# Output projection of the attention layer: by head group inside the last query chunk instead of a stage of its own

## The chip, the cores and the metric

The kernel runs on one core of one Trainium2 chip, in one launch. The metric is device time in microseconds. The engines are named as in the profile: PE is TensorE (PEld its weight loads), DVE is VectorE, ACT is ScalarE, POOL is GpSimd, SP is SyncE, which here issues most of the DMAs.

## The reference

A graph network of four layers on 3327 nodes with 128 features. `adj` is a dense 3327 x 3327 matrix of zeros and ones. Every layer adds its result to x after a layer norm and a relu:

```python
h = relu(layernorm(x)); x = x + L0(h, adj)        # two rounds of swish(adj @ h @ W + b)
h = relu(layernorm(x)); x = x + L1(h, adj)        # attention, below
h = relu(layernorm(x)); x = x + L2(h, adj)        # adj @ h, then a GRU cell
h = relu(layernorm(x)); x = x + L3(h, adj)        # two Laplacian products, with 4 nearest neighbours added

def L1(x, adj):                                   # d = 128 "heads" of width h = 8, n = 3327
    q = (x @ Wq.T).reshape(d, n, h)               # k and v alike
    a = einsum('dnh,dmh->dnm', q, k) * d ** -0.5
    a = softmax(a + adj + adj, axis=2)
    out = einsum('dnm,dmh->dnh', a, v)
    return out.reshape(n, h * d) @ Wo.T           # the output projection
```

The reshapes are plain: they don't transpose. The result of head d at query n therefore stands at position d * 3327 + n of one long row, and row r of the reshaped matrix takes 128 positions of that row. So four heads in a row give about 104 whole rows of the projection (103 or 104), and these rows are complete as soon as the four heads have all their queries.

## The kernel before

Almost all of the time is the attention, some 480 to 10036 us of the span. It is cut into seven query chunks of 476 columns (the last, chunk 6, has 471), each of these into 32 groups of four heads, each group into 26 tiles of 128 keys. Tiles are taken in blocks: in chunks 1 to 6 eight triples and one pair to a group. The order of all engines is written out by hand in this part: instructions go to each engine's queue in the order in which the loops emit them.

One block does these steps, in the order that a string gives (`ORDERS`):

- `a`, `A`, `b`, `B`, `c`: score products on PE (`Block.product`, L926) into one of two pairs of PSUM banks (`banks.pair`, which take turns; `c` fills one bank of a pair), and behind each step a sum on DVE (L942) that adds the adjacency tile and writes `p_early`. A letter is two heads of one tile, `c` a single head. When the last sum of a block is queued, one exponential on ACT over all of them follows (L947).
- `l`: three heads of the last tile into the PSUM tile `late`, an exponential on ACT straight from there (L956), and a product with exp(adj) on POOL (L958).
- `W`: weighing (L969), the product of the probabilities with the values, of a tile that lies about seven tiles back, accumulated in the bank `acc`. After a group's last tile DVE copies `acc` to `o4` (L980) and SP stores it to `ot` in DRAM (L985): eight rows of weighted sums and a ninth with the softmax's denominators.

Blocks alternate between two orders; a triple has `aWAWbWBlc` or `cWaWAbWlB`. Since a group has nine blocks, groups alternate too. `events` (L1009) is called after each block for each of its tiles and emits what comes along: the next group's q and v loads at tile 8 (`load_rest`), the next keys at tile 4, in earlier chunks the next chunk's adjacency columns, and POOL's sums of adjacency columns for the degrees.

After the attention comes `tail`, whose order is left to the framework's planner, not written out; the planner may place an instruction far from its place in the program. `tail` first does the output projection in 26 steps: load `o` from `ot`, reciprocal of the denominators (L1187), product (L1188), eight transposes on PE (L1193), copies on ACT (L1194), eight fp32 products with `wo` (L1197, two instructions each), sum with x in `xs_late` (L1198). Pieces of the layer norm (`layernorm_relu`, in pieces given by `CUTS` = 0, 4, 13, 26) follow as their slots are done. Then `adj_product` multiplies with the adjacency matrix (L235), and the GRU cell follows. In `xs_late` row p * 26 + t of x lies in partition p, slot t. The degrees are read (L1202), scaled (L1203) and turned into scale factors (`scales`) between the two. `tail(True)` is a second version for general inputs, in a loop that runs zero times here.

In layer 1's projections (`for r in range(T)`) the column sums of the adjacency's first chunk are made with five products of one column each (`sum_columns`, L304) and stored element by element (`store_sums`).

Of the kernel before, what the change touches and what calls it, by code (L numbers as in the profile page):

```python
# [56 lines left out]
def kernel(  # L57
# [94 lines left out]
    def layernorm_relu(pool, then=None, tmp=None):  # L152
# [20 lines left out]
        return h, in_pieces(piece)  # L173
# [97 lines left out]
    adj16 = dpool.tile([T, P, N], BF16, name="adj16")  # L271
    keyd = dpool.tile([NH // 4, P, NP], F16, name="keyd")
# [243 lines left out]
    for n, t in enumerate(order):  # L516
        kp = rows_of(t)
        if t in kept:
            part_products(acc, n, parts1, t, kept[t], range(len(CS)), False)
            src = kept[t][:kp, : q_chunks[0][1]]  # L520
        else:
            a = early_a.pop(0) if early_a else load_a(t)
            part_products(acc, n, parts1, t, words(a)[:, :, 1], range(len(CS)), False)
            src = a[:kp, : q_chunks[0][1]]
        firsts[t] = doubled(adj_pools[0], src, t, q_chunks[0][1])
        add_to_sum(firsts[t], 0, n == 0)
        if n == 0:
            nc.vector.tensor_reduce(x_max, x1.rearrange("p t d -> p (t d)"), AX.X, ALU.max, apply_absolute_value=True)
        if n == 1:
            bit_limits()  # L530
            nc.gpsimd.dma_start(vd[N * NH : N * NH + 1, :], zero[:1, :EA])
            for end in (qf, kf):
                nc.gpsimd.dma_start(end[:E, N * NH :], zero[:E])
# [42 lines left out]
    class Parting:  # L576
# [8 lines left out]
        def load(self, side):  # L585
            src = SIDES[side][0]
            self.raw[side] = kq0.tile([E * JW, WJ], F32, name="raw")
            nc.sync.dma_start(self.raw[side], self.rows(src, 0))

        def part(self, side, i):  # L590
            if i == 0:
                self.hi[side] = kq0.tile([E * JW, WJ], F16, name="hi")
                self.lo[side] = kq0.tile([E * JW, WJ], F16, name="lo")
# [10 lines left out]
        def at(self, t):  # L604
# [6 lines left out]
            if t == 10:  # L611
                self.load(1)

# [178 lines left out]
    for r in range(T):  # L792
# [30 lines left out]
        if r == 1:  # L823
            dp = ps.tile([P, 512], F32, name="tp")
# [47 lines left out]
    with tc.tile_pool(name="at_in", bufs=1) as a_pool, tc.tile_pool(name="at_p", bufs=4) as p_pool, tc.tile_pool(  # L872
# [114 lines left out]
        with tc.manual_schedule(engines=engines), ExitStack() as ctx_ps:  # L987
# [21 lines left out]
            def events(c, g, t, n, a_in):  # L1009
                nonlocal coming, part, ahead_part, n_stored, k_next  # L1010
                more = n < len(groups)
                if t == 8 and more:
# [30 lines left out]
            coming = part = None  # L1043
            for n, (c, g) in enumerate(groups, 1):
# [10 lines left out]
                for i, size in enumerate(TRIPLES if c else PAIRS):  # L1055
# [9 lines left out]
                    for step in order:  # L1065
# [26 lines left out]
    nc.sync.dma_start(xs, x1d)  # L1092
# [11 lines left out]
    nc.vector.tensor_add(b_rz, b_ih_s, b_hh_s)  # L1104
# [50 lines left out]
    def tail(general):  # L1155
# [13 lines left out]
        with ExitStack() as s:  # L1169
# [6 lines left out]
            h, done = layernorm_relu(pool, halved)  # L1176
            with tc.tile_pool(name="lo", bufs=3) as lo, tc.tile_pool(name="lo_ps", bufs=2, space=PSUM) as ps:
                wo_s = lo.tile([NH, E, D], F32, name="wo_s", bufs=1)
                nc.gpsimd.dma_start(wo_s, wo)
                for t in range(T):  # L1180
                    kp = rows_of(t)
                    o = lo.tile([P, EA, NH], F32, name="o")
                    src = ot.rearrange("e (p t c) -> t p e c", t=T, c=NH)[t]
                    for p0, p1 in ((0, kp),) if kp == P else ((0, 112), (112, kp)):
                        nc.sync.dma_start(o[p0:p1], src[p0:p1])
                    inv = lo.tile([P, NH], F32, name="inv")
                    nc.vector.reciprocal(inv[:kp], o[:kp, E, :])  # L1187
                    nc.vector.tensor_mul(o[:kp, :E, :], o[:kp, :E, :], inv[:kp].unsqueeze(1).to_broadcast([kp, E, NH]))  # L1188
                    oT = lo.tile([NH, E, P], F32, name="oT")
                    for quad in range(2):  # L1190
                        tp = ps.tile([P, 4, P], F32, name="tp")
                        for j in range(4):
                            nc.tensor.transpose(tp[:, j, :kp], o[:kp, 4 * quad + j, :], ident[:kp, :kp])  # L1193
                        nc.scalar.copy(oT[:, 4 * quad : 4 * quad + 4, :kp], tp[:, :, :kp])  # L1194
                    yp = ps.tile([P, D], F32, name="yp")
                    for e in range(E):
                        nc.tensor.matmul(yp[:kp], oT[:, e, :kp], wo_s[:, e, :], start=(e == 0), stop=(e == E - 1))  # L1197
                    nc.vector.tensor_add(xs[:kp, t, :], xs[:kp, t, :], yp[:kp])  # L1198
                    done(t + 1)

            if not general:
                nc.sync.dma_start(deg, degd.rearrange("o (p t) -> (o p) t", t=T))  # L1202
                nc.vector.tensor_scalar_mul(deg, deg, 0.5 / S_SCALE)  # L1203
                nc.vector.tensor_add(deg[:, T - 1 : T], deg[:, T - 1 : T], last_row)
            d1 = inv_sqrt(pool, deg, "d1")
            d1_in, d1_out = d1, d1
            if not general:
                d1_in, d1_out, into4, back4 = scales(pool, d1)

# [6 lines left out]
            with tc.tile_pool(name="l2_tp", bufs=1, space=PSUM) as tps:  # L1216
# [10 lines left out]
                while left:  # L1227
                    transpose_quad(1)
            yT = pool.tile([P, NP], F32, name="yT")
# [377 lines left out]
```

## Time and profile before

| what | value |
|---|---|
| median of 3 runs | 10759.31 us (10756.81 to 10760.92) |
| the profiled execution's own time | 10759.11 us |
| its span, first to last instruction | 10757.4 us |
| busy: PE, DVE, ACT, POOL | 91%, 94%, 92%, 68% |
| chunk 6, first to last o copy | 8723.4 to 10036.4 us |
| output projection in the tail | 10036 to 10141 us |
| next adjacency product | 10145.5 to 10221.3 us |

Times in the profile are microseconds from the span's start. A line of the groups gives line, engine, operation, output and inputs by tile name, shape and count, then busy time, mean length in ns, and the idle time of the engine ahead of them with what ended it. A line of the timeline gives start, length, engine, line, operation and, in brackets, the idle time before it. Consecutive instructions of one engine overlap at their ends, so the distance of two starts is the better measure of what one costs.

### The profile page before, as it was taken

What the parts mean: (1) busy time and instruction counts of PE and PEld (TensorE: products, weight loads), DVE (VectorE), ACT (ScalarE), POOL (GpSimd) and SP (SyncE); (2) the same over time, 40 slices, a digit from 0 to 9 for tenths busy, and PEclk for the clock granted to TensorE, in tenths of its full rate; (3) what the DMA queues carried; (4) which work ended last, traced back from release to release, by engine and by line L of the source; (5) the groups of instructions that cost most, each with busy time, mean ns of one, the idle gap of its engine ahead of it and who ended that gap; (6) DMA issues with size and microseconds to landing.
All of it is one profiled execution on the core that took longest, in us unless ns stands there. A gap on an engine that the chain in (4) does not pass through costs nothing. (4 is left out here: it accounts for less than half of the span.)

```text
span 10757.4 us, 183790 instructions
## 1 busy us (share of the span) xinstructions
PE 9785.6 (91%) x74235; PEld 2140.8 (20%) x74268; DVE 10089.7 (94%) x11602; ACT 9935.9 (92%) x4716; POOL 7294.7 (68%) x3314
## 2 busy tenths in 40 slices
PE   7899999999989999899999999999999989999897
PEld 3211111111111111111111111111111111111453
DVE  5799999999999999999999999999999999999666
ACT  2799999999999999999999999999999999999432
POOL 3388887777777777777777777777777766666203
PEclk9999999999999999999999999999999999999998
DMA  8644433111111111111111111111111111111422
GB/s 294 205 105 104 103 99 87 45 42 45 45 42 45 44 44 43 45 45 43 46 44 44 42 45 46 42 45 43 43 42 44 46 36 38 35 37 38 160 92 101
DMA packets 462641, 709.21 MB, mean 66 GB/s; under 512 B 56587, under 2 KB 391419, under 8 KB 456150
## 3 DMA queue, kind: packets, MB, share of 16 engines
q1 hardware_dynamic: 458596, 690.86, 21.7%
q8 instruction: 585, 9.58, 0.4%
q0 software_dynamic: 3184, 6.51, 0.2%
q14 instruction: 276, 2.26, 0.1%
HBM read 557.43 MB, written 139.73 MB: 65 GB/s over the span
## 5 line engine op out<-in xcount | busy, mean ns | idle before, releaser
L942 DVE TENSOR_TENSOR p_early<-early,a 128x952 f32<-128x952 f32 (+3 forms) x10336 | 9151.8, 957 | 172.3 <-PE early L926 141.3
L947 ACT ACTIVATE p_early<-p_early 128x4284 f32<-128x4284 f32 (+3 forms) x2144 | 8123.9, 3789 | 8.9 <-DVE p_early L942 8.5
L958 POOL TENSOR_TENSOR p_late<-p_late,e 128x1428 f32<-128x1428 f32 (+3 forms) x2144 | 6397.6, 2984 | 2521.4 <-ACT p_late L956 2505.8
L969 PE MATMUL acc<-p_early,v 128*9 128x476 f32 (+3 forms) x33728 | 5704.9, 565 | 126.7 <-issue 114.4
L956 ACT ACTIVATE p_late<-late 128x1428 f32<-128x1428 f32 (+1 forms) x2144 | 3908.6, 1823 | 12.4 <-DMA vd<-v_st 5.3
L926 PE MATMUL early<-q,k_in 32*128 32x476 f16 (+1 forms) x14784 | 3058.5, 366 | 440.1 <-DVE p_early L942 417.3
L969 PE MATMUL acc<-p_late,v 128*9 128x476 f32 (+3 forms) x12864 | 2101.0, 565 | 0.2 <-POOL p_late L958 0.2
L926 PEld LDWEIGHTS <-k_in 32*128 32x128 f16 x19968 | 764.9, 91 | 5446.0 <-issue 5425.1
L926 PE MATMUL late<-q,k_in 32*128 32x476 f16 (+1 forms) x5184 | 778.5, 367 | 178.8 <-ACT p_late L956 178.6
L969 PEld LDWEIGHTS acc<-p_early,v 128*9 128x9 f32 (+1 forms) x33728 | 655.6, 88 | 1197.1 <-issue 1038.7
L926 PE MATMUL early<-q,k 32*128 32x476 f16 x2080 | 395.6, 368 | 6.9 <-DVE p_early L942 5.2
L969 PEld LDWEIGHTS acc<-p_late,v 128*9 128x9 f32 (+1 forms) x12864 | 240.5, 88 | 458.4 <-issue 363.0
L235 PE MATMUL agg_ps<-a,part 128*128 128x512 bf16 (+1 forms) x1067 | 240.8, 378 | 53.1 <-issue 47.4
L926 PEld LDWEIGHTS <-k 32*128 32x128 f16 x3328 | 121.3, 91 | 786.5 <-issue 770.5
L194 ACT ACTIVATE agg<-agg_ps 128x512 f32<-128x512 f32 x9 | 4.7, 598 | 256.6 <-PE agg_ps L235 256.6
L358 PE MATMUL agg_ps<-a,part 128*128 128x512 bf16 (+4 forms) x720 | 171.1, 395 | 56.6 <-DMA a<-in_adjT_dram 55.3
L666 DVE TENSOR_REDUCE k<-k_in 128x256 f16<-128x256 f16 x377 | 221.8, 588 | 0.0
L285 POOL TENSOR_SCALAR a<-a_in 128x476 bf16<-128x476 f32 (+2 forms) x156 | 219.0, 1404 | 0.5
L597 POOL TENSOR_TENSOR lo<-raw,hi 96x278 f16<-96x278 f32 (+1 forms) x256 | 182.3, 712 | 20.5
L296 POOL TENSOR_TENSOR deg_half<-deg_half,a 128x476 f32<-128x476 f32 (+1 forms) x175 | 191.9, 1096 | 2.1
L955 PE MATMUL late<-a,two_i 128*128 128x476 bf16 x544 | 182.2, 373 | 0.0
L1386 PE MATMUL sp<-yT,hT 128*128 128x512 f32 (+1 forms) x364 | 171.3, 612 | 11.6 <-ACT agg L1391 5.7
(289 smaller groups left out, 2693.2 us busy)
## 6 DMA issues: line engine op xcount, KB each, us to landing
k_in<-keyd SPq DMA_DIRECT2D x192, 832.0 KB
v<-vd SPq DMA_DIRECT2D x896, 117.0 KB
a<-in_adjT_dram SPq DMA_DIRECT2D x39, 1663.5 KB
a<-adj SPq DMA_DIRECT2D x78, 831.8 KB
a_in<-in_adjT_dram SPq DMA_DIRECT2D x125, 238.0 KB
keyd<-k SPq DMA_DIRECT2D x416, 64.0 KB
k_in<-kt SPq DMA_DIRECT2D x240, 104.0 KB
q<-qt SPq DMA_DIRECT2D x1520, 14.9 KB
```

Source lines behind the costliest of these rows:

```text
L235: nc.tensor.matmul(acc[c][:, :w], part[:, t, :], a[:, c0 : c0 + w], start=(t == 0 and i == 0), stop=(t == T - 1 and i == len(parts) - 1),)
L285: nc.gpsimd.tensor_scalar(a2[:kp, :w], a, 2.0 * S_SCALE, None, op0=ALU.mult)
L296: nc.gpsimd.tensor_tensor(deg_half[:, :w], deg_half[:, :w], a2[:, :w], op=ALU.add)
L597: nc.gpsimd.tensor_sub(self.lo[side][:, p], raw, hi)
L666: nc.vector.tensor_reduce(k, src.unsqueeze(3), AX.X, ALU.max)
L926: return nc.tensor.matmul(sp[:, : self.we], self.keys(self.t0 + pos)[r], self.q4[r, : self.we], start=True, stop=stop)
L942: Block.first_sum = nc.vector.tensor_tensor(p, scores, a2, op=ALU.add)
L947: nc.scalar.activation(p, p, AF.Exp, scale=1.0 / S_SCALE)
L955: nc.tensor.matmul(late[:, i, :we], two_i, self.a[pos][:, :we], start=False, stop=True)
L956: nc.scalar.activation(self.late[:, :, :we], late[:, :, :we], AF.Exp, scale=1.0 / S_SCALE)
L958: nc.gpsimd.tensor_tensor(g, g, self.e[:, :we].unsqueeze(1).to_broadcast([P, self.n_g, we]), op=ALU.mult)
L969: nc.tensor.matmul(acc[32 * i : 32 * i + EA, :w], self.v4[:kp, i, t, :], p[:kp, :w], start=(t == 0), stop=(t == T - 1),)
```

## The change

The output projection is taken out of the tail (for this kind of input) and done in chunk 6, by head group. A class `Rows` stands for the rows that group g completes: `r0` to `r0 + m`, m being 103 or 104.

- While group g + 1 runs, after its tile 8: SP loads the `ot` rows and the x rows (from `x1d`), in two pieces each (96 rows and the rest); the tiles that `Parting` used in chunk 0 (`raw`, and `parts` in place of `hi` and `lo`) are used again for this. After tile 17 DVE makes the reciprocal; after tiles 17 and 20 POOL multiplies by it, four of the eight parts each time.
- While group g + 2 runs, in its block 0 behind step `A`: eight transposes on PE into the next pair of banks, one copy of both banks on DVE (`turn`). In block 2 behind step `A`: eight products with `wo` on PE into the next pair, the sum with x on DVE, and the store of the new x rows to `yo` in DRAM by SP (`project`).
- The last two groups' rows are done behind the last block: `turn` of group 30 before the remaining weighings, `project` after them, then all of group 31 in a row, with the division on DVE.
- `wo` is loaded at group 0 of chunk 6 into eight tiles that held keys in chunk 0. In chunk 6 the next group's q and v loads move from tile 8 to tile 14.
- The tail loads `xs_late` from `yo` in five pieces (`X_CUTS` = 0, 2, 6, 12, 19, 26), with the layer norm cut alike. The reading of the degrees, `scales` and the sum `b_rz` stand behind `adj_product` in the program.
- The first chunk's column sums are made as one row (`ones` as the stationary side), copied and stored as a row.

```diff
+    yo = dpool.tile([NP, D], F32, name="yo")
...
+    class Rows:
+        def __init__(self, g):
+            self.r0 = 4 * g * N // NH
+            self.m = 4 * (g + 1) * N // NH - self.r0
+            self.pieces = ((0, 96), (96, self.m))
+        def load(self):
+            self.o = kq0.tile([P, EA * NH], F32, name="raw").rearrange("r (e c) -> r e c", c=NH)
+            rest = kq0.tile([P, 2, WJ + 1], F16, name="parts").bitcast(F32).rearrange("p a b -> p (a b)")
+            m = self.m
+            self.oT, self.y, self.inv = rest[:, : E * m], rest[:m, E * m : E * m + D], rest[:m, E * m + D : E * m + D + NH]
...
+            for p0, p1 in self.pieces:
+                nc.sync.dma_start(self.o[p0:p1], src[self.r0 + p0 : self.r0 + p1])
+                nc.sync.dma_start(self.y[p0:p1], x1[self.r0 + p0 : self.r0 + p1])
+        def invert(self):
+            nc.vector.reciprocal(self.inv, self.o[: self.m, E, :])
+        def divide(self, engine, e0, n):
+            o = self.o[: self.m, e0 : e0 + n]
+            engine.tensor_tensor(o, o, self.inv.unsqueeze(1).to_broadcast([self.m, n, NH]), op=ALU.mult)
+        def turn(self, tp):
+            m = self.m
+            for e in range(E):
+                nc.tensor.transpose(tp[:, e // 4, e % 4 * m : (e % 4 + 1) * m], self.o[:m, e, :], ident[:m, :m])
+            nc.vector.tensor_copy(self.oT.rearrange("c (a r) -> c a r", a=2), tp[:, :, : 4 * m])
+        def project(self, yp, wo_s):
+            m = self.m
+            for e in range(E):
+                nc.tensor.matmul(yp[:m, 0, :D], self.oT[:, e * m : (e + 1) * m], wo_s[e], start=(e == 0), stop=(e == E - 1))
+            nc.vector.tensor_add(self.y, self.y, yp[:m, 0, :D])
+            for p0, p1 in self.pieces:
+                nc.sync.dma_start(yo[self.r0 + p0 : self.r0 + p1], self.y[p0:p1])
...
         if r == 1:
-            end = sum_columns(0, dp)
-            sums = l1.tile([P, 512], F32, name="deg_sums", bufs=1)
-            for n, c0, c1 in ((SUM_ROWS, QW, end - 1), (QW % SUM_ROWS, end - 1, end)):
-                nc.vector.tensor_copy(sums[:n, c0:c1], dp[:n, c0:c1])
-            store_sums(0, sums)
+            nc.tensor.matmul(dp[:1, :w], ones, deg_half[:, :w], start=True, stop=True)
+            deg_row = l1.tile([1, QW], F32, name="deg_row", bufs=1)
+            nc.vector.tensor_copy(deg_row[:, :w], dp[:1, :w])
+            nc.sync.dma_start(degd[:, :w], deg_row[:, :w])
...
-                if t == 8 and more:
+                if t == (8 if c + 1 < len(q_chunks) else 14) and more:
                     coming = first[n] if n < len(first) else load_rest(*groups[n])
...
+                if c + 1 == len(q_chunks) and g == 0 and t == 2:
+                    for e in range(E):
+                        k = kq0.tile([P, 2, P], F16, name="k", bufs=KEYS_AHEAD + 1)
+                        wo_s.append(k.bitcast(F32).rearrange("p a b -> p (a b)"))
+                        nc.sync.dma_start(wo_s[e], wo[:, e, :])
+                if c + 1 == len(q_chunks) and g:
+                    if t == 8:
+                        rows = Rows(g - 1)
+                        rows.load()
+                    if t == 17:
+                        rows.invert()
+                    if t in (17, 20):
+                        rows.divide(nc.gpsimd, 0 if t == 17 else 4, 4)
...
                             block.sums(pos, which, c > 0)
+                        if step == "A" and rows and i == 0:
+                            rows.turn(banks.pair()[0])
+                        if step == "A" and rows and i == 2:
+                            rows.project(banks.pair()[0], wo_s)
+                            rows = None
...
+            rows.turn(banks.pair()[0])
             while to_weigh:
                 weigh_next()
+            rows.project(banks.pair()[0], wo_s)
+            rows = Rows(n_groups - 1)
+            rows.load()
+            rows.invert()
+            rows.divide(nc.vector, 0, E)
+            rows.turn(banks.pair()[0])
+            rows.project(banks.pair()[0], wo_s)
             for a in to_store:
                 store_adj(*a)
...
-    nc.sync.dma_start(xs, x1d)
...
-    nc.vector.tensor_add(b_rz, b_ih_s, b_hh_s)
...
-            h, done = layernorm_relu(pool, halved)
+            h, done = layernorm_relu(pool, halved, cuts=CUTS if general else X_CUTS)
+            if not general:
+                by_slot = yo.rearrange("(p t) d -> p t d", t=T)
+                for t0, t1 in zip(X_CUTS, X_CUTS[1:]):
+                    nc.sync.dma_start(xs[:, t0:t1], by_slot[:, t0:t1])
+                    done(t1)
+            else:
...
                 adj_product(agg, h, parts, transpose_quad)
                 while left:
                     transpose_quad(1)
             if not general:
                 nc.sync.dma_start(deg, degd.rearrange("o (p t) -> (o p) t", t=T))
                 nc.vector.tensor_scalar_mul(deg, deg, 0.5 / S_SCALE)
...
+            nc.vector.tensor_add(b_rz, b_ih_s, b_hh_s)
```

More of the change, by code (lines that the diff above doesn't have):

```diff
@@ L150, in in_pieces, with layernorm_relu @@
         return done
-    def layernorm_relu(pool, then=None, tmp=None):
+    def layernorm_relu(pool, then=None, tmp=None, cuts=CUTS):
         h = pool.tile([P, T, D], F32, name="h")
@@ L171, in piece @@
                 then(h, p, n)
-        return h, in_pieces(piece)
+        return h, in_pieces(piece, cuts)
     def load_rows(dst, src, t, col0, w):
@@ L531 @@
             nc.gpsimd.dma_start(vd[N * NH : N * NH + 1, :], zero[:1, :EA])
+            nc.gpsimd.dma_start(yo[N:], zero[:1, :D])
             for end in (qf, kf):
@@ L586, in load @@
             src = SIDES[side][0]
-            self.raw[side] = kq0.tile([E * JW, WJ], F32, name="raw")
+            self.raw[side] = kq0.tile([P, EA * NH], F32, name="raw")[: E * JW, :WJ]
             nc.sync.dma_start(self.raw[side], self.rows(src, 0))
@@ L591, in part @@
             if i == 0:
-                self.hi[side] = kq0.tile([E * JW, WJ], F16, name="hi")
-                self.lo[side] = kq0.tile([E * JW, WJ], F16, name="lo")
+                parts = kq0.tile([P, 2, WJ + 1], F16, name="parts")
+                self.hi[side], self.lo[side] = (parts[: E * JW, j, :WJ] for j in range(2))
             p = slice(i * W4, min((i + 1) * W4, WJ))
@@ L612, in at @@
                 self.load(1)
+    class Rows:
[8 more added lines that the diff above has]
+            self.oT, self.y, self.inv = rest[:, : E * m], rest[:m, E * m : E * m + D], rest[:m, E * m + D : E * m + D + NH]
+            src = ot.rearrange("e (r c) -> r e c", c=NH)
+            x1 = x1d.rearrange("p t d -> (p t) d")
+            for p0, p1 in self.pieces:
[18 more added lines that the diff above has]
+                nc.sync.dma_start(yo[self.r0 + p0 : self.r0 + p1], self.y[p0:p1])
     PARTING_TILES = (6, 7, 8, 9, 16, 17, 18, 19)
@@ L823 @@
         if r == 1:
+            w = q_chunks[0][1]
             dp = ps.tile([P, 512], F32, name="tp")
[L825 to L829 removed]
+            nc.tensor.matmul(dp[:1, :w], ones, deg_half[:, :w], start=True, stop=True)
+            deg_row = l1.tile([1, QW], F32, name="deg_row", bufs=1)
+            nc.vector.tensor_copy(deg_row[:, :w], dp[:1, :w])
+            nc.sync.dma_start(degd[:, :w], deg_row[:, :w])
             nc.sync.dma_start(degd[:, N:], zero[:1, :1])
@@ L1009, in events @@
             def events(c, g, t, n, a_in):
-                nonlocal coming, part, ahead_part, n_stored, k_next
+                nonlocal coming, part, ahead_part, n_stored, k_next, rows
                 more = n < len(groups)
-                if t == 8 and more:
+                if t == (8 if c + 1 < len(q_chunks) else 14) and more:
                     coming = first[n] if n < len(first) else load_rest(*groups[n])
@@ L1041, in events @@
                         to_store.append((c + 1, i, a_next[-1]))
-            coming = part = None
+            coming = part = rows = None
+            wo_s = []
             for n, (c, g) in enumerate(groups, 1):
@@ L1174, in halved @@
                 split_unless_general(parts, h, p, scale=PART)
-            h, done = layernorm_relu(pool, halved)
[L1177 to L1199, printed above, removed]
@@ L1201, in tail @@
-            if not general:
[L1202 to L1208, printed above, removed]
+            h, done = layernorm_relu(pool, halved, cuts=CUTS if general else X_CUTS)
@@ new lines, in tail @@
+            if not general:
+                by_slot = yo.rearrange("(p t) d -> p t d", t=T)
[3 more added lines that the diff above has]
+            else:
+                with tc.tile_pool(name="lo", bufs=3) as lo, tc.tile_pool(name="lo_ps", bufs=2, space=PSUM) as ps:
+                    wo_s = lo.tile([NH, E, D], F32, name="wo_s", bufs=1)
+                    nc.gpsimd.dma_start(wo_s, wo)
+                    for t in range(T):
+                        kp = rows_of(t)
+                        o = lo.tile([P, EA, NH], F32, name="o")
+                        src = ot.rearrange("e (p t c) -> t p e c", t=T, c=NH)[t]
+                        for p0, p1 in ((0, kp),) if kp == P else ((0, 112), (112, kp)):
+                            nc.sync.dma_start(o[p0:p1], src[p0:p1])
+                        inv = lo.tile([P, NH], F32, name="inv")
+                        nc.vector.reciprocal(inv[:kp], o[:kp, E, :])
+                        nc.vector.tensor_mul(o[:kp, :E, :], o[:kp, :E, :], inv[:kp].unsqueeze(1).to_broadcast([kp, E, NH]))
+                        oT = lo.tile([NH, E, P], F32, name="oT")
+                        for quad in range(2):
+                            tp = ps.tile([P, 4, P], F32, name="tp")
+                            for j in range(4):
+                                nc.tensor.transpose(tp[:, j, :kp], o[:kp, 4 * quad + j, :], ident[:kp, :kp])
+                            nc.scalar.copy(oT[:, 4 * quad : 4 * quad + 4, :kp], tp[:, :, :kp])
+                        yp = ps.tile([P, D], F32, name="yp")
+                        for e in range(E):
+                            nc.tensor.matmul(yp[:kp], oT[:, e, :kp], wo_s[:, e, :], start=(e == 0), stop=(e == E - 1))
+                        nc.vector.tensor_add(xs[:kp, t, :], xs[:kp, t, :], yp[:kp])
+                        done(t + 1)
@@ L1228, in tail @@
                     transpose_quad(1)
+            if not general:
+                nc.sync.dma_start(deg, degd.rearrange("o (p t) -> (o p) t", t=T))
+                nc.vector.tensor_scalar_mul(deg, deg, 0.5 / S_SCALE)
+                nc.vector.tensor_add(deg[:, T - 1 : T], deg[:, T - 1 : T], last_row)
+            d1 = inv_sqrt(pool, deg, "d1")
+            d1_in, d1_out = d1, d1
+            if not general:
+                d1_in, d1_out, into4, back4 = scales(pool, d1)
+            nc.vector.tensor_add(b_rz, b_ih_s, b_hh_s)
             yT = pool.tile([P, NP], F32, name="yT")
```

## The prediction

> **What bounds the kernel now.** I read the page first (10757.4 us of span, ScalarE 92% and VectorE 94% busy), then the windows by stage, because the change takes work out of the tail and puts it into the last chunk of the attention.
>
> ```profile
> core 0: us, PE busy (x) PEld busy (x) DVE busy (x) ACT busy (x) POOL busy (x), PEclk, DMA share, GB/s
> 9000.00:9400.00 400.00, 364.67 (x2956) 67.32 (x2959) 393.15 (x417) 400.00 (x172) 274.21 (x95) 1.00 0.12 37
> 10036.00:10141.00 105.00, 84.23 (x628) 76.86 (x624) 72.20 (x103) 33.75 (x61) 6.75 (x14) 0.90 0.59 177
> ```
>
> In chunk 6 ScalarE never rests (400.00 of 400) and VectorE nearly never. The projection stage after it, 105 us, has no engine full. So what is moved goes from a stage with room into one without. How much room there is, the groups by shape for 8700 to 10000 say:
>
> ```profile
> line engine op names shapes xcount | busy us, mean ns | idle before us <-releasers
> L942 DVE TENSOR_TENSOR p_early<-early,a 128x944 f32<-128x944 f32 x1041 | 1114.3, 1133 | 19.6 <-PE early L926 17.8
> L947 ACT ACTIVATE p_early<-p_early 128x4248 f32<-128x4248 f32 x245 | 1050.4, 4287 | 5.4 <-DVE p_early L942 5.4
> ...
> L942 DVE TENSOR_TENSOR p_early<-early,a 128x472 f32<-128x472 f32 x276 | 166.4, 640 | 1.7
> ...
> L980 DVE COPY o<-acc 105x471 f32<-105x471 f32 x30 | 19.1, 638 | 0.0
> ```
>
> Instructions of one engine overlap by some 0.08 us, so by their starts a double sum costs VectorE 1.05 us, a single one 0.56, the o copy 0.56. A triple is 4 x 1.05 + 0.56 = 4.76, the last pair of a group 2.66: a group is 8 x 4.76 + 2.66 + 0.56 = 41.3 us. On ScalarE the exponentials of a triple start 3.63 and 1.24 apart (4.87), of the pair 3.30: 42.26. The o copies (L980) come 42.65 and 41.92 us apart in turn, 42.28 in the mean: ScalarE sets the pace and VectorE has 1.0 us a group to spare. That there is no stock to live on, one hole in the chunk's first group shows:
>
> ```profile
> 8734.89 0.91 DVE L1203 TENSOR_SCALAR deg<-deg 128x26 f32<-128x26 f32 x1 [4.59 <-DMA deg<-degd]
> 8737.49 3.74 ACT L947 ACTIVATE p_early<-p_early 128x4248 f32<-128x4248 f32 x1 [4.97 <-DVE p_early L942]
> ```
>
> 5.5 us lost on VectorE, and ScalarE lost 5.9 (4.97, 0.74 and 0.20); that group took 49.29 us, the next few gave back 0.6.
>
> **What is removed.** The tail's rows:
>
> ```profile
> 10036.40 0.65 DVE L980 COPY o<-acc 105x471 f32<-105x471 f32 x1 [7.44 <-PE acc L969]
> 10040.80 0.95 DVE L1187 RECIPROCAL inv<-o 128x128 f32<-128x128 f32 x1 [3.75 <-DMA o<-ot]
> 10041.79 1.22 DVE L1188 TENSOR_TENSOR o<-o,inv 128x1024 f32<-128x1024 f32 x1
> ...
> 10043.12 1.94 PE L1193 MATMUL tp<-ident,o 128*128 128x128 f32 x8 [6.78 <-DVE o L1188]
> 10045.01 4.09 PE L1197 MATMUL yp<-wo_s,oT 128*128 128x128 f32 x16
> ...
> 10065.95 1.04 PE L1193 MATMUL tp<-ident,o 128*128 128x128 f32 x8
> 10067.28 2.05 PE L1197 MATMUL yp<-wo_s,oT 128*128 128x128 f32 x16 [0.29 <-ACT oT L1194]
> ...
> 10145.50 0.59 PE L235 MATMUL agg_ps<-a,part 128*128 128x512 bf16 x1 [1.01 <-DMA a<-adj]
> ```
>
> From the last weighing's end (10036.34) to the first adjacency product are 109.2 us. The product itself (10145.5 to 10221.3) stays: 14 matmuls of about 0.21 a tile.
>
> **What is left there.** Group 31 can only be projected after its own weighing, all in series. From that end: o copy 0.7; four stores issued, 2.2; landed 4.2 (2 us, as the output's 1.93); o read, 442 KB after 4.2 us for 576 KB above, 8.0; reciprocal and division 10.3; eight transposes at the slow clock (1.94) 12.3; copy of 832 wide, 1.0, 13.3; 16 matmuls, between 2.05 and 4.09, 16.4; add 0.3, 16.7; stores of yo issued 17.4. Behind them on SP comes the left-over adj16 store; before, it went out at 10038.60 and xs_late's load waited until 10043.41 for it. I take 21.5 for both to land, 24 for the first piece of xs_late. Its layernorm (two slots) is six VectorE and three ScalarE steps of 0.2 to 0.45, a table load of 1.28 and their hops: 29.5. The first adjacency tile is issued after the xs_late pieces (6 x 0.37) and needs 4.4 (10141.07 to 10145.50), longer behind 1.7 MB of x: 28 to 34. I take 31, plus 2.5 for the clock: **33.5, so 109.2 - 33.5 = -76** (ends -68 and -83). The later pieces of layernorm, 16 us of VectorE, lie beside 76 us of products; without that cover they would cost 16.
>
> The clock row: eight transposes took 1.94 us after 6.78 us of idle and 1.04 once warm, the matmuls 4.09 against 2.05. The Trainium skill, "TensorE: Matmul & The Clock Gate", section on what is actually happening, lets the array fall to half clock after an idle window of about 3.4 us and return after as long a busy one. That speaks against the change, whose end is short bursts between DMAs; by it every burst there and the product's first 3.4 us run at half clock, an estimate of 2 us more than mine.
>
> **What is added in chunk 6.** Per group, 104 rows: reciprocal 0.86 (L1187, by starts), copy out of PSUM 832 wide 0.93 (L980's 0.56 for 471, and some 360 more at the 0.49 that 472 more cost a sum), add 0.20 (L1198): **1.99 us of VectorE**. 41.3 + 1.99 = 43.25 is over ScalarE's 42.26: VectorE becomes the bound, +0.97. TensorE gets 8 transposes at 0.11 (0.86) and 16 matmuls at 0.11 (1.75); it is 365 of 400 busy, so the sum fits, but both stand whole in its queue behind step A of blocks 0 and 2, and take a turn of the two score pairs. VectorE then has one sum left to live on. I laid the queues of blocks 0 and 2 out by these durations (a product 0.30 to the next weighing, a weighing 0.91, 0.05 from end to start; the old order so laid gives 42.66 and 41.93). In a group whose blocks run aWAWb, from the start of A's sum: TensorE gets its pair at 0.13, is through project at 1.88, readable at 2.10; VectorE was done at 1.05, idle **1.05**. Then the weighing that ends the old group, 0.91, must end before the o copy: idle **0.79**; the new group's first weighing waits for that copy and B's products with it: **0.41**. At turn in block 0: 0.16, then 0.18 and 0.16 at b and B. With 0.51 at the group's end this makes 3.26. In the other group (cWaWAb: b's products follow at once) 0.49 and 0.31 at project, 0.16 at turn, 0.14: 1.10. Mean 2.2 of idle: a group takes 43.25 + 2.2 = 45.4, **+3.1**, and groups 2 to 31 have both steps: **30 x 3.1 = +93**. Group 1 has only the reciprocal, inside the 1.0. Ends: 0.97 if no idle is left (+29); 4.0 if what both engines get falls in series (0.86 + 1.75 + 1.99 + two hops, less 1.0; +120). I stay near the middle of the layout, since it repeats the old periods.
>
> **At nothing, with its cover.** POOL's divisions, 1.16 each (L958: 3.22 for 1416), lie in its 1.65 us of idle per triple; a weighing of a late part comes 7 tiles later; without that it would wait 1.2. SP gets six DMAs a group (2.4 us) and waits some 2 us for the old yo store before y; behind it come the next q and v, now at tile 14 instead of 8: 6.9 us of issue with 12 tiles (19 us) until use; if that cover fails, each group waits for q. The wo tiles: 8 issues, 2.8 us, in a lull. Turn of group 30 goes ahead of the last weighings, which have 1.6 us of gaps (0.57, 0.74, 0.25): +0.5. The degree row in layer 1 turns ten small matmuls into two and two copies of 0.15 into one of some 0.6, where VectorE waits for ScalarE: 0, ends -0.5 and +0.5. deg's load and scaling are moved in the program, but the trace has them at 8732, long ahead of their place: I leave the 5.9 us where they are; ends 0 and -6. yo's zeros are one POOL issue in layer 0: 0.
>
> **Sum.** 93 + 0.5 - 76 = +17.5 on the profiled execution's 10759.1 (span 10757.4 and 1.7 around it; the median of the three is 10759.3): **10777**.
>
> **Rivals.** *Slower:* each insertion stalls fully; TensorE's change from 32-row products to full matmuls and the semaphores add to both steps, and a group costs 4.0: +120 - 76 = +44, 10803. It decides from 3.25 us a group on (30 x 3.25 - 76 = 21.5). For it: the hole of 5.5 that cost 5.9. Against: the project in every second group finds a product of b right behind it. *Faster:* the stalls fall into waits that are there anyway (VectorE's 0.70 idle a group, ScalarE-bound), leaving the arithmetic: 30 x 0.97 + 0.5 - 76 = -46, 10713. Against: TensorE does not look ahead past project, and the two pairs hold one sum. *It does not do what it says:* the adjacency tiles or xs_late still wait for another release, the tail gives 50 instead of 76: 10803.
>
> **Chances.** Forecast case, a group at +2.6 to +3.6 and the tail within its ends, 10760 to 10798: 0.70, of which 0.40 lies within 0.2% (21.5 us, about what a measurement of this kernel can tell from no change) and 0.30 above. Slower rival 0.10, failing tail 0.04, faster rival 0.16. Faster 0.16, within 0.2% 0.40, slower 0.44. The range 10736 to 10806 leaves out most of the faster rival and the far end of the slower one, less than 0.2.
>
> **What would show it.** Chunk 6's o copies 47.5 and 43.2 us apart in turn (45.4 mean); ScalarE under 94% there, with waits for p_early; VectorE idle before the add about 1 us in every second group; first L235 some 33 us after the last weighing; no group of L1187 in the tail. Groups at 43.3 would refute the stalls, 46.3 prove the first rival; a gap over 45 us after the weighing would refute the tail's term.

## The result and the profile after

The changed kernel takes 10786.92 us (median of 13 runs, 10785.17 to 10791.71) against 10756.12 us before (13 runs beside it): a ratio of 1.0029, 95% interval 1.0022 to 1.0037. It is slower by 0.29%. The forecast was 10777, with "slower by over 0.2%" as the likeliest of the three answers (0.44).

The span of the profiled execution grew by 29.3 us, from 10757.4 to 10786.7. Three marks cut that up: the first copy of attention outputs out of PSUM (the "o copy", L980 before and L1022 after), the first o copy of chunk 6, and the last one.

| stretch | before | after | difference | forecast |
|---|---|---|---|---|
| start to first o copy | 484.5 | 476.7 | -7.8 | 0 |
| to first o copy of chunk 6 | 8239.0 | 8238.1 | -0.8 | 0 |
| to last o copy | 1313.0 | 1428.3 | +115.3 | +93.5 |
| to the end | 721.0 | 643.6 | -77.4 | -76 |

The windows of the same two stages as before, chunk 6 and what stands in place of the projection stage (the columns are busy time and count of each engine, then the granted TensorE clock, the DMA share and GB/s):

```profile
core 0: us, PE busy (x) PEld busy (x) DVE busy (x) ACT busy (x) POOL busy (x), PEclk, DMA share, GB/s
9000.00:9400.00 400.00, 361.31 (x2919) 82.81 (x2917) 380.69 (x409) 372.82 (x158) 273.80 (x105) 0.99 0.17 48
10143.70:10175.20 31.50, 7.21 (x39) 6.08 (x37) 9.33 (x24) 3.36 (x7) 5.49 (x10) 0.56 0.65 212
```

In chunk 6 ScalarE, 400.00 of 400 before, is now 372.82: it is no longer the bound. But VectorE is less busy too (380.69 against 393.15), and TensorE's clock is not whole. So no engine is full: they wait for one another. The stage of 105 us has become 31.5 us in which every engine mostly waits for DMAs. The groups by shape of chunk 6 name the new work and the new waits:

```profile
line engine op names shapes xcount | busy us, mean ns | idle before us <-releasers
L984 DVE TENSOR_TENSOR p_early<-early,a 128x944 f32<-128x944 f32 x959 | 1029.4, 1132 | 27.3 <-PE early L968 25.6
...
L646 DVE COPY parts<-early 128x832 f32<-128x832 f32 x28 | 28.7, 1025 | 6.0 <-PE early L645 5.1
L636 DVE RECIPROCAL parts<-raw 104x128 f32<-104x128 f32 x28 | 26.4, 943 | 0.0
L1022 DVE COPY o<-acc 105x471 f32<-105x471 f32 x28 | 18.0, 643 | 9.1 <-PE acc L1011 9.1
L652 DVE TENSOR_TENSOR parts<-parts,early 104x128 f32<-104x128 f32 x27 | 7.8, 288 | 20.3 <-PE early L651 20.3
```

Less the 0.08 of overlap, copy, reciprocal and add cost 0.94, 0.86 and 0.21, in all 2.01 us a group; the forecast had 1.99. What surprises is in the last column: the o copy never waited before (0.0 of 30), now it waits 9.1 us, and the add 20.3. A stretch of VectorE's timeline at the project step of an aWAWb group shows where:

```profile
9044.76 0.29 DVE L652 TENSOR_TENSOR parts<-parts,early 104x128 f32<-104x128 f32 x1 [1.04 <-PE early L651]
9045.69 0.65 DVE L1022 COPY o<-acc 105x471 f32<-105x471 f32 x1 [0.65 <-PE acc L1011]
9046.26 1.13 DVE L984 TENSOR_TENSOR p_early<-early,a 128x944 f32<-128x944 f32 x1
9047.77 15.95 DVE L984 TENSOR_TENSOR p_early<-early,a 128x944 f32<-128x944 f32 x17 [0.38 <-PE early L968]
```

These are the three waits that the forecast laid out: 1.05, 0.79 and 0.41 there, 1.04, 0.65 and 0.38 here.

The o copies come 43.27, 48.12, 43.27 and 49.69 us apart, and so on in rounds of four: 46.09 in the mean, +3.81 on 42.28. (The first distance, which also holds VectorE's wait for deg, grew from 49.29 to 55.15.) The fourth of each round was not forecast. There TensorE runs at half clock. Four windows, each of 3.41 us: the first pair at an undisturbed turn, the second pair at a disturbed one:

```profile
9212.02:9215.43 3.41, 2.38 (x25) 0.52 (x19) 2.91 (x4) 3.41 (x2) 3.10 (x1) 1.00 0.42 107
9215.43:9218.84 3.41, 2.81 (x28) 1.07 (x26) 3.18 (x4) 3.34 (x3) 2.05 (x1) 1.00 0.36 147
9304.18:9307.59 3.41, 1.78 (x16) 0.38 (x13) 3.41 (x4) 3.41 (x2) 2.33 (x1) 1.00 0.67 217
9307.59:9311.00 3.41, 3.41 (x18) 1.45 (x18) 1.88 (x2) 2.57 (x2) 2.82 (x1) 0.50 0.08 33
```

The transposes of these two turns, on TensorE's timeline:

```profile
9216.16 0.91 PE L645 MATMUL early<-ident,raw 104*128 104x104 f32 x8 [0.60 <-DVE p_early L984]
...
9307.55 1.58 PE L645 MATMUL early<-ident,raw 104*128 104x104 f32 x8 [0.60 <-DVE p_early L984]
```

In the windows, the first number after the length is TensorE's busy time. It waits twice near the turn, 1.03 and 0.60 us. In the first pair a window holds one wait each, and the clock stays at 1.00. In the second pair both fall into one window (3.41 - 1.78 = 1.63 idle), and the next window has 0.50: there the eight transposes take 1.58 instead of 0.91 us and VectorE stands for them. Seven such stretches lie 184.3 us apart, the length of four groups; one more lies in the chunk's first group, at 8744.39.

The tail, from the last o copy on:

```profile
10143.10 0.65 DVE L1022 COPY o<-acc 105x471 f32<-105x471 f32 x1 [5.45 <-PE acc L1011]
10143.78 1.35 SPq L1027 DMA_DIRECT2D ot<-o  x4
...
10153.70 0.95 DVE L636 RECIPROCAL parts<-raw 104x128 f32<-104x128 f32 x1 [8.41 <-DMA raw<-ot]
10154.68 1.23 DVE L640 TENSOR_TENSOR raw<-raw,parts 104x1024 f32<-104x1024 f32 x1
...
10156.01 1.62 PE L645 MATMUL early<-ident,raw 104*128 104x104 f32 x8 [11.05 <-DVE raw L640]
...
10158.75 3.74 PE L651 MATMUL early<-k,parts 128*104 128x128 f32 x16 [1.12 <-DVE parts L646]
...
10165.38 2.25 SPq L1247 DMA_DIRECT2D xs_late<-yo  x5
...
10165.92 1.28 POOL L111 DMA_DIRECT2D w_s<-in_w_dram  x2 [24.23 <-DMA adj<-a]
...
10171.51 0.31 ACT L1190 ACTIVATE w_sq<-w_s 128x128 f32<-128x128 f32 x1 [4.31 <-DMA w_s<-in_w_dram]
10171.73 0.40 ACT L165 ACTIVATE ln_sq<-ln_xc 128x256 f32<-128x256 f32 x1
...
10172.16 0.42 DVE L166 TENSOR_REDUCE ln_var<-ln_sq 128x2 f32<-128x256 f32 x1 [2.72 <-ACT ln_sq L165]
...
10174.74 0.40 ACT L219 ACTIVATE part<-h 128x256 f16<-128x256 f32 x1
...
10175.19 0.13 PEld L235 LDWEIGHTS <-part 128*128 128x128 f16 x2 [0.33 <-ACT part L219]
10175.19 1.03 PE L235 MATMUL agg_ps<-a,part 128*128 128x512 bf16 x2
```

From the last weighing's end (about 10143.0) to the first adjacency product are 32.2 us; before they were 109.2. The bracket of 8.41 is the round trip of the last group through DRAM. What the first product waits for is the first piece of the layer norm (L219), and that was held up by a load: ScalarE stands 4.31 us for w_s, a tile of weights, the squares of the layer norm stand behind it in its queue, and VectorE waits 2.72 us for them.

### The profile page after: what moved, and what is told of

Read it like the earlier page. It is cut to its first block, busy times and chain, and to the rows that moved or that the text cites. A ratio compares the mean times of both kernels' runs of the same rounds, so it can differ in the third digit from the quotient of the medians.

```text
span 10786.7 us, 184465 instructions
## 1 busy us (share of the span) xinstructions
PE 9785.6 (91%) x74404; PEld 2148.1 (20%) x74404; DVE 10103.1 (94%) x11634; ACT 9928.6 (92%) x4670; POOL 7370.4 (68%) x3376
## 5 line engine op out<-in xcount | busy, mean ns | idle before, releaser
L989 ACT ACTIVATE p_early<-p_early 128x4284 f32<-128x4284 f32 (+3 forms) x2144 | 8013.9, 3738 | 22.2 <-DVE p_early L984 19.1
L998 ACT ACTIVATE p_late<-late 128x1428 f32<-128x1428 f32 (+1 forms) x2144 | 3801.1, 1773 | 93.9 <-PE early L968 57.5
L359 PE MATMUL agg_ps<-a,part 128*128 128x494 bf16 (+5 forms) x728 | 168.0, 389 | 54.0 <-DMA a<-in_adjT_dram 53.2
L599 POOL TENSOR_TENSOR parts<-raw,parts 96x278 f16<-96x278 f32 (+1 forms) x256 | 182.4, 712 | 20.5
```

Of the source, the lines that this page charges most:

```text
L599: nc.gpsimd.tensor_sub(self.lo[side][:, p], raw, hi)
L989: nc.scalar.activation(p, p, AF.Exp, scale=1.0 / S_SCALE)
L998: nc.scalar.activation(self.late[:, :, :we], late[:, :, :we], AF.Exp, scale=1.0 / S_SCALE)
```

## The experiments

A "group" below is the mean distance of o copies in the middle of chunk 6: 42.28 us before, 46.09 in the changed kernel.

**The two insertions left out (none).**

```
-   if step == "A" and rows and i == 0:
-       rows.turn(banks.pair()[0])
    if step == "A" and rows and i == 2:
-       rows.project(banks.pair()[0], wo_s)
+       rows.store()          # y as loaded, without the projection
        rows = None
```

> The changed kernel, in which the groups inside chunk 6 load, invert, divide and store their rows as before but leave out the turn (8 transposes and the copy) and the project (16 products and the add); the output lacks the attention part of these rows. It gives the price of the two insertions. Theory: what costs is VectorE's work and the score pairs' turns, so with VectorE at 41.3 + 0.86 = 42.2 us a group ScalarE bounds again: a mean group of 42.3 to 42.9 us, and 10787 less 30 x (46.1 - 42.6) = 10682 us, within 10. The half-clock stretches of every fourth group go with it. Rival: the rows' own loads, stores and divisions (the SP queue, POOL) carry part of the cost: groups above 44 us and a time above 10720.

10692.86 us, ratio 0.9940 (0.9927 to 0.9954); groups of 42.19 and 43.30 in turn, 42.74. The windows view of chunk 6:

```profile
9000.00:9400.00 400.00, 360.63 (x2925) 65.56 (x2921) 394.96 (x421) 397.09 (x170) 295.99 (x114) 1.00 0.19 52
```

ScalarE is back at 397.09 and the clock at 1.00. So of the 3.81 us that a group lost, turn and project carry 3.35, and the rows' loads, stores, divisions and reciprocal 0.46 together. The group fits the theory; the time is 1 us past its edge. Moving the stage would be worth 63 us if the insertions cost nothing.

**TensorE's share of them (few).** Two half-precision products replace the eight transposes, one product (two matmul instructions) the eight:

```
-   for e in range(E): transpose(tp[...], o[:m, e, :], ident)
+   for j in range(2): matmul(tp[:, j, : 4 * m], k[:, :P], k[:, : 4 * m])
...
-   for e in range(E): matmul(yp[:m, 0, :D], oT[...], wo_s[e])
+   for e in range(1): ...
```

> The changed kernel, in which a row group inside chunk 6 is turned with 2 half-precision products of 416 columns in place of 8 transposes, and projected with 1 product pair in place of 8 (its result is not the attention's); VectorE's copy, add and reciprocal and the two turns of the score pairs stay. Theory: about half of what a group is longer than in the kernel named none (46.1 against 42.7 us) is VectorE's arithmetic (copy and add, 1.13 us) and half TensorE's clump of transposes and products, for which VectorE waits; with the clump gone a group comes to 44.2 us (43.9 to 44.6) and the time to 10787 - 30 x 1.9 = 10730 us. Rival: the turns of the pairs themselves cost, whatever is written there: 45.5 us and more, 10770 and more.

10748.47 us, 0.9989 (0.9980 to 0.9998). Undisturbed groups take 43.14 and 45.78, 44.46, within the expected bounds; with a few half-clock stretches the mean is 44.70. The time came out 18 us above what was expected: chunk 6 became 42.5 us shorter (1428.3 to 1385.8) and not 57, because undisturbed groups are 0.26 us longer than the 44.2 of that sum and the stretches add 0.24, and in the two profiles the rest of the kernel took some 6 us more. In the changed kernel the undisturbed groups take (43.27 + 48.12) / 2 = 45.70, so what was taken out of TensorE's clump is worth 1.24 us of each group; VectorE's instructions and the turns of the pairs are left with the rest.

**Where the results are written (late).**

```
-   if step == "A" and rows and i == 0: rows.turn(banks.pair()[0])
+   if step == "A" and rows and i == 1: rows.turn(ps.tile([P, 3, 512], F32, name="late")[:, :2])
-   if step == "A" and rows and i == 2: rows.project(banks.pair()[0], wo_s)
+   if step == "b" and rows and i == 2: rows.project(ps.tile([P, 3, 512], F32, name="late"), wo_s)
```

> The changed kernel with turn and project written into the tile of the late scores (three banks that ScalarE reads straight, one tile) instead of a turn of the two score pairs: turn after step A of the second block, project after step b of the third. Instructions and sizes are the same. Theory: of the 46.1 us a group only 43.25 are VectorE's work; the rest is its waiting because a pair is taken away. Without that a group comes to 44.3 to 45.0 us and the time to 10787 - 30 x 1.4 = 10745 us (10733 to 10757). Rival: the late tile is a single one, so the late products wait for the copy and the add, ScalarE's late exponentials come late, and the group is as long as now or longer (46 us and more, 10785 and more).

10760.22 us, 1.0004 (0.9995 to 1.0013): no different from before. Undisturbed groups of 44.38 and 45.48, 44.93, inside the expected 44.3 to 45.0, and in the middle of the chunk one half-clock stretch (two windows long) instead of seven. The same instructions in the same engines cost 1.16 us a group less when they take no turn of the score pairs (0.39 of it is the clock). Their place in the queue changed too; move, below, changes the place alone and leaves undisturbed groups at 45.87, but late's own places were not tried with the pairs. VectorE's timeline shows what is left:

```profile
9171.04 0.28 DVE L652 TENSOR_TENSOR parts<-parts,late 104x128 f32<-104x128 f32 x1
9172.28 15.39 DVE L984 TENSOR_TENSOR p_early<-early,a 128x944 f32<-128x944 f32 x16 [0.97 <-PE early L968]
```

The add no longer waits; the scores after it do, 0.97 us, since they stand behind the 16 matmuls and the weighings in TensorE's queue. The time missed its expected range by 3 us.

**The reciprocal taken off VectorE (late_pool, late_newton).** First as a power on GpSimd, then as Newton steps there:

```
late_pool:   gpsimd.tensor_tensor(inv, o[:m, E, :], minus_one, op=ALU.pow)
late_newton: gpsimd.tensor_scalar(inv as int32, o[:m, E, :] as int32, -1.0, 0x7EF311C7, mult, add)
             3 times: d = x * inv; d = 2 - d; inv = inv * d      (gpsimd)
             divisions at tiles 20 and 23 instead of 17 and 20
```

> As the kernel named late, and the reciprocal (0.86 us of VectorE per group) taken as a power of -1 on GpSimd. Theory: VectorE's work falls to 42.4 us a group, next to ScalarE's 42.3; a group comes to 43.5 to 44.2 us, and the time to 10745 - 30 x 0.8 = 10721 us (10710 to 10735), below the kernel before. Rival: the power on GpSimd, which no row of the profile prices, takes several us, holds the late products' multiplications behind it, and the weighings wait: no better than late, or worse.

11248.93 us, 1.0458: the rival, and how. GpSimd's timeline:

```profile
9054.03 20.73 POOL L641 TENSOR_TENSOR parts<-raw,minus 104x128 f32<-104x128 f32 x1
9074.83 1.26 POOL L645 TENSOR_TENSOR raw<-raw,parts 104x512 f32<-104x512 f32 x1
9076.05 3.17 POOL L1005 TENSOR_TENSOR p_late<-p_late,e 128x1416 f32<-128x1416 f32 x1
```

The power takes 20.73 us, the late products behind it wait, then the weighings: some 60 us a group.

> As the kernel named late (44.9 us a group, 10760 us), and the reciprocal of 0.86 us taken from VectorE: GpSimd makes a first guess from the bits of the denominator and betters it in three Newton steps (10 short instructions over 104 x 128, spread over two stretches of the group), and its divisions come one block later. Theory: VectorE stays the bound, a group falls by 0.6 to 0.86 us to 44.1 to 44.3 us, and the time to 10760 - 30 x 0.7 = 10739 us (10733 to 10745), below the kernel before by 0.16%. Rival: GpSimd's queue holds the late products' multiplications, as the power did: 10760 and more.

10750.33 us, 0.9992 (0.9983 to 1.0001); groups of 44.14 and 44.68, 44.41. The ten short GpSimd instructions (0.30 to 0.46 each) hold nothing up, so the rival is wrong, but a group fell by only 0.52 us of the 0.86, and the time is 5 us above the expected range. VectorE's gaps grew from 1.38 to 1.61 us a group: those behind TensorE's project remain (0.97 and 0.93 in turn), and one of 0.42 ahead of the turn's copy, in every second group, is new.

**The degree's scaling on GpSimd (deg_pool).** It adds to late_newton:

```
-   nc.vector.tensor_scalar_mul(deg, deg, 0.5 / S_SCALE)
-   nc.vector.tensor_add(deg[:, T - 1 : T], deg[:, T - 1 : T], last_row)
+   nc.gpsimd.tensor_scalar_mul(...); nc.gpsimd.tensor_add(...)
```

> As late_newton (44.4 us a group, 10750 us), with the scaling of the degree and the addition of the last row on GpSimd instead of VectorE, where the scaling stood 4.8 us for the degree's load in the first group of chunk 6 (50.2 us). Theory: GpSimd stands for it in place of VectorE, which keeps its scores; the first group falls by 4 to 5.5 us to about 45.5, and the time to 10745 us (10743 to 10748), 0.12% below the kernel before. Rival: GpSimd's stop holds two late products' multiplications, the weighings wait for these and the group is as long as now: 10750.

10737.99 us, 0.9982 (0.9973 to 0.9991), 0.18% faster than the kernel before, with an interval that leaves out 1, and 5 us below the expected range; the changed kernel beside it took 10789.44. GpSimd's timeline in the first group:

```profile
8731.10 0.29 POOL L1306 TENSOR_SCALAR deg<-deg 128x26 f32<-128x26 f32 x1 [5.04 <-DMA deg<-degd]
8731.48 0.19 POOL L1307 TENSOR_TENSOR deg<-deg,last_row 128x1 f32<-128x1 f32 x1
8731.63 6.42 POOL L1010 TENSOR_TENSOR p_late<-p_late,e 128x1416 f32<-128x1416 f32 x2
```

GpSimd stands for 5.04 us, catches up with two late products at once, and no one else notices: the first group falls from 50.23 to 43.44 and chunk 6 from 1382.1 to 1375.2. These 6.9 us are the edit's. Of the rest between the two profiles, deg_pool is 5.1 ahead at the start of chunk 6, where nothing was changed, and 1.9 behind after it. The edit has nothing to do with the projection: the kernel before has the same wait (4.59 us), and no run tried the edit there.

**The half-clock stretches (fill, move).**

```
fill:  if order == "aWAWbWBlc" and rows and i == 0:
           5 score products into the late tile ahead of the first step, 3 ahead of the turn
move:  turn at i == 2, project at i == 3, rows loaded at tile 11
```

> The changed kernel with score products added where TensorE waits next to the turn in every second group (5 ahead of the first block, 3 ahead of the turn; each 0.2 us after the one before, into the late scores' tile, which the block's own late products overwrite). Theory: the seven stretches of 3.4 us at a granted clock of 0.5, one in every fourth group of 49.7 us, come because TensorE stands idle for 1.03 and 0.60 us shortly before; with these waits filled they vanish, these groups fall to 48.1 us, and the time falls by 7 x 1.57 = 11 us to 10776 (10771 to 10781). Rival: the stretches are set by something else (the transposes themselves, or a fixed beat): they stay, and the time is within 3 us of 10787 or longer by the products' own time.

10861.71 us, 1.0095: neither holds, by a fault in the experiment. TensorE's timeline:

```profile
9244.71 0.57 PE L968 MATMUL late<-q,k_in 32*128 32x472 f16 x5 [3.82 <-ACT p_late L998]
```

The late tile was still held by the last block's exponentials, and the products that were to fill a wait of 1.03 us made one of 3.82. Every second group now holds one or more stretches at 0.50. It tells nothing of a kernel with less waiting, only that more of it brings more of them.

> The changed kernel with the turn in the third block of the group and the project in the fourth (both after step A, each in a turn of the score pairs), the rows loaded one block later. In the changed kernel the waits of TensorE of 1.03 us (start of the first block) and 0.60 us (ahead of the turn) lie within 3 us of each other in every second group, and the seven stretches at a granted clock of 0.5 follow when both fall into one 3.41 us window. Theory: apart, the two waits leave the clock alone: no stretch at 0.5 within the groups of chunk 6, no group of 49.7 us, a mean group of 45.4 to 45.9 us and a time of 10770 to 10782. Rival: the stretches come with the eight transposes wherever they stand: they stay, one in every fourth group or more, and the time is 10785 or longer.

10793.98 us, 1.0032 (1.0020 to 1.0044), as slow as the changed kernel beside it (10789.44, 10783 to 10796). Undisturbed groups of 44.00 and 47.73 (45.87) are as expected, but a stretch came in every sixth group, neither never nor in every fourth, and the time is 12 us above the theory's. The windows around one:

```profile
8834.45:8837.86 3.41, 2.16 (x18) 0.44 (x18) 3.41 (x5) 3.34 (x2) 3.41 (x2) 1.00 0.09 26
8837.86:8841.27 3.41, 3.38 (x16) 0.46 (x19) 2.64 (x3) 3.27 (x2) 2.80 (x2) 0.50 0.56 145
```

Here 1.25 us of idle was enough, without the pairing that I had supposed. All stretches of one execution lie on one grid of 3.41 us. I sorted the windows of that grid from 8750 to 10080 us by TensorE's idle time in the matmul records, for the twelve profiles other than fill and late_pool: of some 740 full-clock windows with 0.6 to 1.1 us idle none was followed by half clock, of 37 with 1.1 to 1.4 ten were, of 32 with 1.4 and more all were. This is seen, not produced on purpose: no run here took the idle time away and left all else.

**The degree row (deg_row, no_deg_row, no_deg_row_again, after_again).** The row alone in the kernel before, and the changed kernel without it:

```
-   end = sum_columns(0, dp)                      (ten small matmuls, two copies, two stores)
+   nc.tensor.matmul(dp[:1, :w], ones, deg_half[:, :w])     (one row, one copy, one store)
```

> The kernel before with the degree row alone: the first chunk's degree sums as one row, everything else as before. My theory (the forecast's term of 0, within 0.5): the time stays within 1 us of before, and the first copy of attention outputs (484.46 us in the profile of before) stays within 2 us. Rival: the 7.8 us that the changed kernel is ahead at that copy (476.68) come from the degree row: then this kernel is 5 to 8 us faster than before.

10750.68 us, 0.9996 (0.9987 to 1.0005).

> The changed kernel with the first chunk's degree sums as before, in two pieces. Theory: the degree row is worth nothing that can be told (0, within 2 us) and the 7.8 us at the first copy of attention outputs are the spread of the part of the kernel that DMA feeds: 10787 within 4 us, and the first copy anywhere from 475 to 485 us. Rival: the row is worth 5 to 8 us: 10792 to 10795 us and a first copy at 482 us or later.

10797.98 us, 1.0037 (1.0023 to 1.0050).

> The kernel no_deg_row once more, beside the changed kernel on the same chip: the two single differences so far (5.6 us faster than before with the row alone, 11 us slower than the changed kernel without it) had no common base. Theory: no difference beyond 3 us. Rival: the row is worth 5 to 10 us, then this kernel is that much slower than after_again.

10793.83 us (10791.65 to 10795.47).

> The changed kernel as it is, for the comparison with no_deg_row_again, move and deg_pool on the same chip: 10787 us within 4, and a first copy of attention outputs anywhere from 475 to 485 us. By the theory that the degree row is worth nothing it agrees with no_deg_row_again within 3 us, by the rival it is 5 to 10 us faster.

10789.44 us (10783.07 to 10795.88), first o copy at 479.1.

All differences have one sign, 5.6, 11 and 4.4 us for the row, beyond what the theory allowed each time. Two of the pairs ran beside each other, deg_row with the kernel before and the last two kernels; their means differ by 4.9 and 4.6 us, each with a standard error of 1.7, and in both pairs the ranges overlap. Eleven profiles with the row reach chunk 6's first o copy at 8713.5 to 8723.6 us, the three without it at 8720.5 to 8723.5; the means are 8717.7 and 8722.5. The first o copy of the kernel is no measure: with the row it lies anywhere from 474.9 to 484.4. So the row is probably worth some 5 us, which the runs show as a difference and not as a cause: no row of a trace names what it saves. How much of the 7.8 us of the two profiles is the row and how much is spread stays open.

## Why the prediction was right, point by point

- **The tail: right in size, not in path.** -76 was said, -77 measured (109.2 to 32.2). Reciprocal and division ended 12.9 us after the last weighing instead of 10.3: the rows' load was issued at 5.3 us, not 4.2, and took longer, though it is 432 KB in the profile's unit and not 442. The 16 matmuls took 3.74, near the upper bound of 4.09. But the adjacency tiles were loaded early, at 10143 and 10150, and not after x, so the load that the forecast put last, at 31 us, held nothing up. The product waited for the first layer norm piece, forecast at 29.5 and done at 32.1, with ScalarE's 4.31 us for w_s ahead of it, which the forecast did not have. So the two errors offset each other, and the 2.5 us added for the clock are shown by no run alone: that the sum came out to 1 us is luck in part. By the estimate from the Trainium skill, "TensorE: Matmul & The Clock Gate", the section on what is actually happening, the half clock was to cost 2 us more than my sum; the clock was indeed 0.56 over this stretch, and the total came out below the sum all the same. From the first product to the end 611.5 us remain, against 611.9 before: the later pieces of the layer norm cost nothing, as said. The last o copy to the end took 640 to 646 us in the twelve profiles with the rows in chunk 6, and 721.0 and 716.9 in the two without.
- **VectorE becomes the bound: the arithmetic right, "bound" too strong.** 2.01 us a group were added, 1.99 forecast. ScalarE fell to 93.2% as said. But no engine is full; the handing over between TensorE and VectorE sets the pace, as the three waits of the layout did.
- **+3.1 us a group was mis-sized: 3.81.** This is the term that failed, and it moved the result from within 0.2% to slower. A little of it is arithmetic: 41.3 + 1.99 is 43.29, not 43.25, and with the 2.18 of idle, less 42.28, the layout gives 3.19 a group, 96 us in all. Undisturbed groups took 45.70 (+3.42). VectorE's gaps in the trace come to 1.91 us a group (3.38 and 0.44 in turn), less than was laid out; but at each gap it also loses the 0.08 us by which its instructions overlap, over some seven gaps 0.54, and 2.45 with 43.3 of work is the group to within 0.1. The other 0.39 is the clock, for which the sum had no term in chunk 6: one group in four is 1.57 us longer. Against 3.1 that is 0.71 a group, 21 us over 30 insertions; 30 x 3.81 and 0.9 of wind-down (39.50 against 38.58 to the last o copy) make the 115.3. In that, the chunk's first distance has +5.9 and the other 29 have 3.74 in the mean. The slower rival named 4.0; its point of decision, 3.25, was passed, and 46.09 lies nearer to the 46.3 that was to prove it than to 45.4. But its reason, that each insertion stalls fully, is not what the rows show, since the cWaWAb group came out as laid (43.27 against 43.2).
- **The total came nearer than its terms, by luck.** Chunk 6 took 21.8 us more than forecast. The 7.8 us at the start, for which the forecast had nothing, and 1.4 us in the tail took some of it back. The other stages alone would have given +37 us against the +17.5 forecast.
- **The faster rival is refuted.** It had the stalls fall into waits that are there anyway, +0.97 a group. few and late together show why not: with the clump smaller, or with the pairs left alone, over 2 us a group remain.
- **What was put at nothing.** GpSimd's divisions, SP's DMAs and the q and v loads are in the 0.46 us of none, with the reciprocal; they were not quite nothing. That this is because neither VectorE (42.2) nor ScalarE (42.3) has stock to pass over the other's waits is an argument, not shown. deg stayed where the trace had it (4.49 us of wait on VectorE at 8726.24), as assumed. The degree row, put at 0 with ends of 0.5, is probably worth some 5 us.

## What to carry to other kernels

When a step is moved into a stage that an engine fills, price its place in the queues and in the buffers before its instructions: here the arithmetic was 2.0 us a group, the price 3.8, and the same instructions cost 1.2 us less in a tile that was not part of the busy engine's double buffer, a little further on in the queue. A load's consumer belongs on the engine with slack: moving a 5 us wait from VectorE to GpSimd gave back 6.9 us. Of the 77 us that the tail gained, the best version is only some 21 ahead of the kernel before, because the stage that took the work in was full; 7 of these come from the degree's scaling and perhaps 5 from the degree row, neither of which needs the projection to be moved.

## What the runs showed of the hardware

- TensorE's granted clock fell to 0.50 for a 3.41 us window after a window in chunk 6 in which it had idled 1.1 to 1.6 us, far less than whole (of the windows with 1.1 to 1.4 us idle, 10 of 37; of those with more, all). The Trainium skill, "TensorE: Matmul & The Clock Gate", the section on what is actually happening, has the clock fall after an idle window; in these traces a window less than half idle was enough, and the measurement decides. The stretch lengthened a group by 1.57 us.
- The group's length and this window locked together: in two profiles of the changed kernel the stretches came every 184.32 us, which is 54 windows of 3.413 us and four groups (43.27 + 48.12 + 43.27 + 49.69 = 184.35). It is no fixed beat: in no_deg_row_again, with the same groups, 549.5 us passed between the first two stretches and 184.3 between the next.
- A power on GpSimd over 104 x 128 took 20.7 us, a product of the same size 0.46 and a multiply-add with two constants 0.30.
